# AdaLN block: one DRAM tile for a head's keys, the first two chunks of projections kept on the chip, residuals through TensorE, and a DMA queue in program order

## The chip, the cores and the metric

The kernel runs on one core of a Trainium2 chip. The metric is the device time of one execution in microseconds (us); the time before is the median of six executions. The core has TensorE (PE; its weight loads are listed apart as PEld), VectorE (DVE), ScalarE (ACT) and GpSimd (POOL); SyncE (SP) issues most of the DMA transfers, one after another from its queue.

## The reference

One transformer block with adaptive layer norm over B = 2 sequences of N = 2048 tokens and D = 256 features; H = 16 heads of 16 features each; E = 8 experts.

```python
mod = silu(c) @ wmod                      # six rows of D per sequence
sa, ca, ga, sb, cb, gb = mod              # ga, gb: sign kept, size at least 0.25
h = layernorm(x) * (1 + ca) + sa
q, k, v = h @ Wq, h @ Wk, h @ Wv          # 16 heads of 16
R_hat = (1 + exp(v_h)) / (1 + exp(v_h - w_h * |i - j|))
scores = relu(q k^T) * R_hat              # causal: -inf above the diagonal
x = x + ga * (softmax(scores / 4) v @ Wo + bo)
h = layernorm(x) * (1 + cb) + sb
p = softmax(h @ gate_w^T)                 # 4096 tokens, 8 experts
idx = top 512 tokens of each expert by p
y = layernorm(h[idx]) * ln_w + ln_b
out = (gelu(y @ fc1^T + b1) @ fc2^T + b2) * p[idx]
h[idx] += out                             # scatter-add
x = x + gb * h
```

All of it is float32 except some masks and counts.

## The kernel before

**Start.** A few loads are followed by the first layer norm and the projections of sequence 0, in four chunks of 512 tokens: `prologue(0, c)` lists the steps (load, statistics, normalisation, transposes, projections of k, q and v). Each projected tile is copied out of PSUM by ACT (L513, L530), and stored to DRAM: `k_d[b][i]` and `q_d[b][i]` are 128 x 512 (eight heads of one chunk; i = 4 times the group of eight heads plus the chunk), `v_d` likewise. What a head needs is loaded back from there, spread to partitions 0, 32, 64 and 96 so that four matmuls of 16 rows can run side by side: `keys` (L566) loads four pieces of 16 x 512 for each of four chunks, 16 transfers for a head, `queries` (L606) four of 16 x 512 for each block of 512 queries, `values` (L572) a `vg` tile shared by four heads, and `head_inputs` (L584) the head's distance table `tb` (128 x 2048, from `rhat_d`, which `distances` writes at L363 and L365).

In the program's order: `table = by_distance()`, the first chunk's statistics and normalisation, dummy transposes (`idle`) and the modulation, `narrow()`, `distances(*table)`, chunk 0's projections and loads, chunk 1's normalisation, chunk 1's projections and loads, 20 more dummy transposes, chunk 2's normalisation. The projections of chunks 2 and 3 are fillers, and so is everything else of the start that head 0 does not need. When chunk 3 has arrived, head 1's inputs are asked for, and `late_loads()` loads the output weights, modulation rows and gate weights.

**Attention.** The order of PE, DVE, ACT and POOL is written out by hand by a planner. It keeps a modelled time for each engine, goes over the units (a head and a block of queries) from the first to the last, and puts fillers between their steps: projections of the second sequence, and the epilogues of finished groups of tokens. `there[c]` is the modelled time at which chunk c is usable, `made[...]` the one at which a piece of filler work is finished, `late(i)` says whether the fillers are behind at unit i, and `over()` whether the last scores have been issued. The engine SP is not in the hand-written order: a scheduler places its transfers. Scores are matmuls of L907 into `sc`; DVE multiplies by the table and takes the row maximum (L920, L927), POOL sets the causal part (L932), PE transposes (L971), ACT takes the exponential (L979), PE multiplies by the values (L1012).

**Epilogue of a group of 512 tokens** (`epilogue(b, g)`, pieces for each of four tiles k): `turn` transposes the context (L660, ACT copy at L662), `project` multiplies by Wo (L669) and `add` adds it to the residual `x1`. Once `over()` holds, the addition is made by DVE straight from PSUM (L675). Then come statistics (L690), the normalisation to `h2` (L715, L751), the gate logits (L771 to L783), the row of `z_d` (L788, L792), and the two products of `base`: `h2` times the modulation row and the sum with `x1`, which POOL does (L625), followed by a store to the output (L765).

**Routing and experts.** The top 512 of each expert are found by a bisection over bits of the score's bit pattern: 15 steps, each with three counts on DVE (L1511), one count matmul `pcnt` on PE (L1516) and the comparisons (L1528 and after). Whatever of the epilogues is still undone lies in `left`: its DVE pieces go into the bisection's steps, its POOL pieces are issued by `rest_of_output()` after expert 0's gathers. Then for each expert, POOL gathers 512 rows (L1656, indirect DMA of `zt`), PE transposes (L1671) and does both matmuls (L1682, L1706), and POOL scatter-adds (L1713).

Of the kernel before, what the change touches and what calls it, by code (L numbers as in the profile page):

```python
# [172 lines left out]
def adaln_block_kernel(  # L173
# [30 lines left out]


    q_d = [[dram.tile([P, 512], FP, name=f"q_d_{b}_{i}") for i in range(HG * 4)] for b in range(B)]
    k_d = [[dram.tile([P, 512], FP, name=f"k_d_{b}_{i}") for i in range(HG * 4)] for b in range(B)]
    v_d = [[dram.tile([512, 8 * VW], FP, name=f"v_d_{b}_{i}") for i in range(HG * 4)] for b in range(B)]


# [235 lines left out]
    def prologue(b: int, c: int, hT, first: bool):  # L446
# [56 lines left out]
        def qk(g: int, w_sb, dst, tag: str, parts: list):  # L503
            n = len(parts) * P
            pp = turned([P, n], f"p{tag}_{u}_{g}_{parts[0]}")
            for k in range(DC):
                nc.tensor.matmul(
                    pp, lhsT=w_sb[:, k, ts(g, P)], rhs=s["hT"][:, k, ds(parts[0] * P, n)],
                    start=(k == 0), stop=(k == DC - 1),
                )  # L510
            if parts[0] == 0:
                s[tag, g] = ev_p.tile([P, 512], FP, name=f"{tag}_{u}_{g}", tag="qk")
            nc.scalar.copy(s[tag, g][:, ds(parts[0] * P, n)], pp)  # L513
            if parts[-1] == 3:
                nc.sync.dma_start(out=dst[b][g * 4 + c], in_=s[tag, g])
            return plan.small(427 * len(parts), 120 + 120 * len(parts), 0)

        def val(g: int, parts: list):
            pv = turned([P, len(parts), P], f"pv_{u}_{g}_{parts[0]}")
            for j, i in enumerate(parts):  # L520
                for k in range(DC):
                    nc.tensor.matmul(
                        pv[:, j, :], lhsT=s["hT"][:, k, ts(i, P)], rhs=wv_sb[:, k, ts(g, P)],
                        start=(k == 0), stop=(k == DC - 1),
                    )
            if parts[0] == 0:
                vt = s["v", g] = ev_p.tile([P, 4, 8, VW], FP, name=f"vt_{u}_{g}", tag="vt", bufs=2)
                nc.gpsimd.memset(vt[:, :, :, HD:VW], 1.0)
            vt = s["v", g]
            nc.scalar.copy(  # L530
                vt[:, ds(parts[0], len(parts)), :, 0:HD],
                pv.rearrange("p k (h f) -> p k h f", f=HD),
            )
# [27 lines left out]
        return work  # L561


    def keys(b: int, h: int, c: int):
        for r in range(RG):
            nc.sync.dma_start(  # L566
                out=inputs[b, h][0][ds(32 * r, HD), ts(c, 512)],
                in_=k_d[b][h // 8 * 4 + c][ts(h % 8, HD), :],
            )

    def values(b: int, h: int, c: int):
        nc.sync.dma_start(  # L572
# [3 lines left out]
            ),  # L576
        )

    def head_inputs(b: int, h: int, chunks=range(4)):
        kr = krp.tile([P, N], FP, name=f"kr_{b}_{h}", tag="kr")  # L580

        tb = tabp.tile([P, N], FP, name=f"tb_{b}_{h}", tag="tab")
        row = rhat_d[h, :]
        nc.sync.dma_start(  # L584
            out=tb, in_=bass.AP(tensor=row.tensor, offset=row.offset, ap=[[1, P], [1, N]])
        )

        if h % 4 == 0:
            vg = vgp.tile([P, NQ * 4 * VW + HD], FP, name=f"vg_{b}_{h}", tag="vg")
            nc.gpsimd.memset(vg[:, NQ * 4 * VW :], 0.0)  # L590
        else:
            vg = inputs[b, h - 1][2]
        inputs[b, h] = (kr, tb, vg)
        for c in chunks:
            keys(b, h, c)
            if h % 4 == 0:
                values(b, h, c)

    def queries(at: int):

        if at >= len(asked):
            return
        b, h, c = asked[at]
        qr = qrp.tile([P, 512], FP, name=f"qr_{b}_{h}_{c}", tag="qr")
        for r in range(RG):
            nc.sync.dma_start(  # L606
                out=qr[ds(32 * r, HD), :], in_=q_d[b][h // 8 * 4 + c][ts(h % 8, HD), :]
            )
        qrs[b, h, c] = qr


    def epilogue(b: int, g: int):
# [52 lines left out]

        def project(k: int):
            po = turned([P, D], f"po_{u}_{k}")
            for f in range(HG):
# [12 lines left out]

        def add_to(k: int):
            if ("added", k) in s:
                return 0.0
            x1 = s["x1"][:, k, :]
            return sum_or_product(x1, s["h2"][:, k, :], x1, ALU.add)

# [33 lines left out]
            skip("widen", k)  # L721
            return plan.small(0, 0, 430)

        def skip(name: str, k: int):
            work[:] = [p for p in work if p[3] != (first, name, k)]
            made[first, name, k] = 0.0

        def root():
            s["root"] = root_of(*s["vr", 3], f"3_{u}")
# [18 lines left out]
        def move(k: int):  # L748
            h2 = s["h2"][:, k, :]
            if ("centered", k) in s:  # L750
                nc.vector.scalar_tensor_tensor(  # L751
                    h2, h2, s["rs2"][:, k : k + 1], sb, ALU.mult, ALU.add
                )
                return plan.small(0, 0, 430)
            return sum_or_product(h2, h2, sb, ALU.add)


        def gated(k: int):
# [59 lines left out]
            work[0][4].extend((first - 4, x, k) for x in ("base", "gate") for k in K)  # L818
        for k in K:
            piece("pe", 218, turn, "turn", k, ("project", k - 2) if k > 1 else ("begin", 0))  # L820
            if g == 3 and k < 2:
                work[-1][4].append((first - 2, "gate", k + 2))
            piece("pe", 853, project, "project", k, "turn", "bias")
# [58 lines left out]
    FIRST_OUT = 11  # L882
    SOON = ("load", "bias", "begin", "turn", "project", "add")
    LOW = ("gated", "base", "rows", "stats3", "power3", "root3", "shift3")
    row_free = [0.0, 0.0]
    OPEN = 4
    groups_out = [[epilogue(b, g) for g in range(4)] for b in range(B)]
# [170 lines left out]
    def divide():  # L1058
# [25 lines left out]
        )  # L1084
        plan.small(0, 0, 200 + 150 * gn)
        if h == H - 1:
            add(groups_out[b][gs[0]][1], False)
            i = turns[-1]["i"] if turns else 0
            more(max(i, H * len(PACKS)), FIRST_OUT * len(PACKS) if b < B - 1 else 12)
# [204 lines left out]

    ENG = mybir.EngineType
    behind = {}
    with tc.manual_schedule(engines={ENG.PE, ENG.DVE, ENG.Activation, ENG.Pool}):
        hT0 = cxp.tile([P, 4, DC, 512], FP, name="hT0", tag="ctx")
        ahead = [prologue(0, c, hT0[:, c, :, :], True) for c in range(4)]

# [52 lines left out]
        table = by_distance()  # L1353
        for _, _, w, *_ in ahead[0][1:6]:
            w()
        for _, _, w, *_ in ahead[0][6:11]:
            w()
        idle(40)
        modulation()
        idle(24)  # L1360
        narrow()
        distances(*table)
        head_inputs(0, 0, [])
        plan.start()
        for c in range(4):
# [28 lines left out]
    def weights(e: int):  # L1394
# [28 lines left out]
    def rest_of_output():  # L1423
        for p in left["pool"]:
            assert all(x in done for x in p[4])
            p[2]()
            done.add(p[3])

    with tc.manual_schedule(engines={ENG.PE, ENG.DVE, ENG.Activation, ENG.Pool}):
        b1_sb = rt.tile([P, E * FC], FP, name="b1_sb")  # L1430
# [12 lines left out]
        nc.gpsimd.iota(steps, pattern=[[0, TOP // 2 + 1], [1, 3]], base=1, channel_multiplier=0)  # L1443
        nc.gpsimd.iota(twice, pattern=[[2, TOP // 2 + 1], [0, 3]], base=0, channel_multiplier=0)
        nc.vector.tensor_tensor(steps, steps, twice, ALU.logical_shift_left)
        thr = rt.tile([P, 1], I32, name="thr0", tag="thr", bufs=2)
        nc.vector.memset(thr, 0)

# [58 lines left out]
        for bit in range(TOP, -1, -2):  # L1507
# [9 lines left out]
            if bit:  # L1517
# [22 lines left out]

        while left["dve"]:
            left["dve"].pop(0)()
            ready_rows()

        hit = rt.tile([P, 2, 2, P], FP, name="hit")
        for k, op in ((0, ALU.is_gt), (1, ALU.is_equal)):
# [258 lines left out]
```

## Time and profile before

| what | value |
|---|---|
| six executions | 1734.68, 1736.26, 1731.92, 1741.42, 1749.59, 1736.20 us; median 1736.23 us |
| the profiled execution's own time | 1724.44 us, 0.68% under the median |
| its span on the chip | 1722.7 us |
| mean granted TensorE clock | 0.949 |
| HBM traffic | 105.82 MB read, 25.70 MB written |

The page's sixth part lists the DMA transfers by kind (form, count, size of one, median us from issue to landing):

```profile
kr<-k_d SPq DMA_DIRECT2D x512, 32.0 KB, 1.9
qr<-q_d SPq DMA_DIRECT2D x512, 32.0 KB, 1.9
vg<-v_d SPq DMA_DIRECT2D x32, 136.0 KB, 3.1
```

The 512 transfers of `kr` are 2 sequences x 16 heads x 4 chunks x 4 groups. The timeline of SP's queue in the start shows chunk 0's keys and queries on their way back from DRAM (start, duration, queue, line, form, count):

```profile
19.85 0.45 SPq L515 DMA_DIRECT2D k_d<-k  x1
20.39 0.47 SPq L515 DMA_DIRECT2D q_d<-q  x1
21.30 0.37 SPq L535 DMA_DIRECT2D v_d<-vt  x1
22.90 0.38 SPq L454 DMA_DIRECT2D xt<-in_x_dram  x1
27.25 1.71 SPq L566 DMA_DIRECT2D kr<-k_d  x4
29.01 2.28 SPq L606 DMA_DIRECT2D qr<-q_d  x4
31.33 0.42 SPq L572 DMA_DIRECT2D vg<-v_d  x1
```

### The profile page before, as it was taken

To read this page: it belongs to the slowest core of one execution; us is meant where nothing else is said; L and a number is where in the kernel's file an instruction comes from. 1 tells how busy PE (TensorE), PEld (TensorE's weight loads), DVE (VectorE), ACT (ScalarE), POOL (GpSimd) and SP (SyncE) were. 2 spreads that over 40 slices of the span, in tenths; PEclk is the share of its full clock that TensorE was granted. 3 is DMA by queue.
4 is the path that set the end of the run, shared out by engine and by line. 5 is a ranking of instruction groups with operands and counts; after the bars stand their busy time and mean duration, and the time that the engine had idled before them with its cause. 6 is when DMAs were issued, how large, how long until landed. Compare 5 with 4: busy or idle time off the path is not lost. (4 is left out here: it accounts for less than half of the span.)

```text
span 1722.7 us, 58026 instructions
## 1 busy us (share of the span) xinstructions
PE 1590.1 (92%) x24205; PEld 1114.5 (65%) x24205; DVE 1320.0 (77%) x2533; ACT 839.9 (49%) x2348; POOL 412.1 (24%) x814
## 2 busy tenths in 40 slices
PE   8999999999999999999999999899999943899997
PEld 6677766676766667666666666566666642567674
DVE  5487798888888787788988998789887777654542
ACT  2455665565655556556665565556555521121211
POOL 1111121211111113122231331313311211834342
PEclk9899999999999999899999999999999955999999
DMA  7432232223222222121221322213220031344431
GB/s 229 98 106 83 70 88 70 71 79 103 72 75 76 75 75 82 53 68 54 73 80 51 91 75 73 85 51 96 58 58 5 18 117 34 98 108 119 112 92 22
DMA packets 111285, 135.31 MB, mean 79 GB/s; under 512 B 43312, under 2 KB 81840, under 8 KB 106928
## 3 DMA queue, kind: packets, MB, share of 16 engines
q1 hardware_dynamic: 104880, 123.08, 24.0%
q0 software_dynamic: 6144, 8.52, 2.9%
q8 instruction: 191, 3.13, 0.8%
q14 instruction: 70, 0.57, 0.1%
HBM read 105.82 MB, written 25.70 MB: 76 GB/s over the span
## 5 line engine op out<-in xcount | busy, mean ns | idle before, releaser
L979 ACT ACTIVATE pt<-tr 128x512 f32<-128x512 f32 (+7 forms) x1628 | 632.7, 457 | 489.5 <-PE tr L971 486.3
L920 DVE CUSTOM_DVE_ANT_0 s<-sc,tb 128x128 f32<-128x128 f32 (+15 forms) x512 | 647.4, 1288 | 207.3 <-PE sc L907 186.3
L971 PEld LDWEIGHTS tr<-ident,s 64*128 64x128 f32 x8704 | 343.4, 141 | 234.0 <-issue 94.2
L971 PE MATMUL tr<-ident,s 64*128 64x64 f32 x8704 | 439.0, 234 | 11.5 <-ACT pt L979 6.3
L932 POOL TENSOR_SCALAR_AFFINE_SELECT s<-s 128x128 f32<-128x128 f32 x512 | 171.7, 349 | 1041.3 <-DVE s L927 615.8
L927 DVE TENSOR_SCALAR s<-s,m 128x128 f32<-128x128 f32 (+15 forms) x512 | 392.1, 792 | 9.1
L907 PE MATMUL sc<-kr,qr 16*128 16x384 f32 (+15 forms) x4096 | 360.0, 443 | 27.7 <-DVE m L920 15.5
L1012 PE MATMUL avb<-pt,vg 128*32 128x128 f32 x8704 | 358.0, 284 | 3.6 <-ACT pt L979 2.9
L1012 PEld LDWEIGHTS avb<-pt,vg 128*32 128x32 f32 x8704 | 230.1, 111 | 65.4 <-issue 21.1
L907 PEld LDWEIGHTS sc<-kr,qr 16*128 16x128 f32 x4096 | 161.1, 188 | 85.5 <-DVE m L920 48.5
L1686 ACT ACTIVATE hT<-ph,b_sb 128x512 f32<-128x512 f32 x64 | 43.9, 687 | 182.7 <-PE ph L1682 182.7
L1682 PE MATMUL ph<-yT,w 128*128 128x512 f32 x256 | 116.7, 600 | 0.9 <-DVE yT L1672 0.5
L1706 PE MATMUL pof<-w,hT 128*128 128x256 f32 x512 | 114.3, 382 | 0.0
L1706 PEld LDWEIGHTS pof<-w,hT 128*128 128x128 f32 x512 | 96.8, 191 | 13.1 <-issue 0.5
L1711 DVE TENSOR_TENSOR o<-pof,b2b 128x256 f32<-128x256 f32 x32 | 13.6, 425 | 89.1 <-PE pof L1706 89.1
L1682 PEld LDWEIGHTS ph<-yT,w 128*128 128x128 f32 x256 | 46.8, 190 | 49.2 <-issue 46.2
L1713 POOL DMA_INDIRECT out_dram<-o,idx x32 | 52.2, 1633 | 94.2 <-DVE o L1712 26.2
L625 POOL TENSOR_TENSOR h<-h,modr 128x256 f32<-128x256 f32 x68 | 51.4, 769 | 0.0
L1656 POOL DMA_INDIRECT zt<-z_d,idx x32 | 33.5, 1047 | 66.4 <-issue 48.7
L261 POOL TENSOR_TENSOR rr<-rv,mhalf 128x4 f32<-128x4 f32 x24 | 24.7, 1029 | 90.6 <-DVE rv L260 90.5
L1028 ACT COPY avs<-avb 128x128 f32<-128x128 f32 x128 | 36.1, 282 | 17.2 <-PE avb L1012 16.1
L1046 PE MATMUL trs<-ident,avs 128*128 128x128 f32 x128 | 42.0, 328 | 1.9 <-ACT avs L1028 0.7
(185 smaller groups left out, 1142.6 us busy)
## 6 DMA issues: line engine op xcount, KB each, us to landing
tb<-rhat_d SPq DMA_DIRECT2D x32, 1024.0 KB, 6.3
kr<-k_d SPq DMA_DIRECT2D x512, 32.0 KB, 1.9
qr<-q_d SPq DMA_DIRECT2D x512, 32.0 KB, 1.9
w<-in_fc1T_dram SPq DMA_DIRECT2D x8, 1024.0 KB, 4.8
w<-in_fc2T_dram SPq DMA_DIRECT2D x8, 1024.0 KB, 5.5
v_d<-vt SPq DMA_DIRECT2D x16, 272.0 KB, 2.4
vg<-v_d SPq DMA_DIRECT2D x32, 136.0 KB, 3.1
xt<-in_x_dram SPq DMA_DIRECT2D x8, 512.0 KB, 4.0
```

The costliest lines, as they stand in the source:

```text
L625: nc.gpsimd.tensor_tensor(out, a, c, op)
L907: nc.tensor.matmul(sc[:, r, ds(at, w)], lhsT=qr[ds(32 * r, HD), ts(q % 4, P)], rhs=kr[ds(32 * r, HD), ts(r, w)], start=True, stop=True,)
L920: nc.vector.tensor_tensor_reduce(out=s[:, ds(RG * at, n)].rearrange("p (r w) -> p r w", w=w), in0=sc[:, :, ds(at, w)], in1=rev, scale=1.0, ...
L927: nc.vector.tensor_scalar(s[:, ds(RG * at, n)], s[:, ds(RG * at, n)], 0.0, m[:, j : j + 1], ALU.max, ALU.subtract,)
L932: nc.gpsimd.affine_select(out=diag, in_=diag, pattern=[[-1, P]], compare_op=ALU.is_ge, fill=MASKED, base=0, channel_multiplier=1,)
L971: nc.tensor.transpose(trs[a][:, at + k, :], u["s"][ts(a, TR), ts(k0 + k, P)], ident[ts(a, TR), ts(a, TR)],)
L979: nc.scalar.activation(u["pt"][:, ds(k0, n), ts(a, TR)], trs[a][:, ds(at, n), :], AF.Exp)
L1012: nc.tensor.matmul(avb[ds(32 * j, 32), grp["slot"], :], lhsT=inputs[b, h][2][:, ds((4 * kt + h % 4) * VW, 32)], rhs=u["pt"][:, k, :], star ...
L1682: nc.tensor.matmul(ph, lhsT=s["w"][0][:, k, ts(f, P)], rhs=s["yT"][:, k, :], start=(k == 0), stop=(k == DC - 1),)
L1686: nc.scalar.activation(s["hT"][:, f, :], ph, AF.Gelu_apprx_tanh, bias=b1_sb[:, e * FC + f : e * FC + f + 1])
L1706: nc.tensor.matmul(po, lhsT=s["hT"][:, f, ts(i, P)], rhs=s["w"][1][:, f, :], start=(f == 0), stop=(f == FC - 1),)
L1713: nc.gpsimd.indirect_dma_start(out=outr, out_offset=bass.IndirectOffsetOnAxis(ap=s["idx"][:, i : i + 1], axis=0), in_=o, in_offset=None, b ...
```

## The change

- `k_d` is one DRAM tile of 128 x 2048 for each group of eight heads, and a head's keys come from it in four transfers of 16 x 2048 instead of sixteen of 16 x 512. In head 0 of sequence 0, whose chunks arrive one by one, chunks 2 and 3 still come as 16 x 512.
- For chunks 0 and 1 of sequence 0, group 0, the projected k, q and v go from PSUM straight into head 0's `kr`, `qr` and `vg` (four copies of 16 x 512 for k and for q, alternately by DVE and ACT; one ACT copy for v) beside the store to DRAM, which the other heads use.
- Chunk 1's projections become a filler; the 20 dummy transposes behind them are gone. `distances` moves ahead of the first normalisation.
- SP joins the engines whose order is that of the program.
- In an epilogue after the last scores, the residual is added by one more matmul with the identity, and ACT copies the sum out; DVE's addition is gone.
- The planner knows when a group's context is finished (`made["context", b, g]`), sets an engine's time to that of the latest thing a filler needs, and treats the fillers as late from unit `PAIR_AT` on.
- Seven of the blocks whose `base` is left at the end go from POOL to PE: a diagonal matrix is made of the modulation row, and in the bisection's steps, `base_turned` transposes a block of `h2` and `base_made` multiplies it by the diagonal and adds `x1` by an identity matmul; ACT copies the result out, SP stores it.

```diff
-    k_d = [[dram.tile([P, 512], FP, name=f"k_d_{b}_{i}") for i in range(HG * 4)] for b in range(B)]
+    k_d = [[dram.tile([P, N], FP, name=f"k_d_{b}_{i}") for i in range(HG)] for b in range(B)]
...
+            if first and g == 0 and c < 2:
+
+                if dst is k_d:
+                    to = inputs[0, 0][0][:, ts(c, 512)]
+                else:
+                    to = qrs[0, 0, c] = qrp.tile([P, 512], FP, name=f"qr_0_0_{c}", tag="qr")
+                for r in range(RG):
+                    (nc.scalar.copy if r % 2 else nc.vector.tensor_copy)(
+                        to[ds(32 * r, HD), :], pp[0:HD, :]
+                    )
...
+    def to_groups(dst: bass.AP, src: bass.AP, h: int):
+
         for r in range(RG):
-            nc.sync.dma_start(
-                out=inputs[b, h][0][ds(32 * r, HD), ts(c, 512)],
-                in_=k_d[b][h // 8 * 4 + c][ts(h % 8, HD), :],
-            )
+            nc.sync.dma_start(out=dst[ds(32 * r, HD), :], in_=src[ts(h % 8, HD), :])
+
+    def keys(b: int, h: int, cs: list):
+        n = 512 * len(cs)
+        to_groups(
+            inputs[b, h][0][:, ds(512 * cs[0], n)], k_d[b][h // 8][:, ds(512 * cs[0], n)], h
+        )
...
+            adds = over()
             for f in range(HG):
                 nc.tensor.matmul(
                     po, lhsT=s["cT", k][:, f, :], rhs=wo_sb[:, b, f, :],
-                    start=(f == 0), stop=(f == HG - 1),
+                    start=(f == 0), stop=(f == HG - 1 and not adds),
                 )
-            if over():
-                x1 = s["x1"][:, k, :]
-                nc.vector.tensor_tensor(x1, po, x1, ALU.add)
-                s["added", k] = True
-                return plan.small(853, 0, 350)
+            if adds:
+                nc.tensor.matmul(po, lhsT=ident, rhs=x1, start=False, stop=True)
+            if adds:
+                nc.scalar.copy(x1, po)
+                there = plan.small(853 + 427, 400, 0)
+                skip("add", k, there)
+                return there
...
+        if not w["in_order"]:
+
+            kind = "dve" if over() and p[0] == "pool" and p[3][1] not in LOW else p[0]
+            if kind in ("dve", "act", "pool"):
+                setattr(plan, kind, max([engine(kind)] + [made[x] for x in p[4]]))
...
-        return ahead_by(i) < (1.5 if plan.now == "f" else -1.5)
+        return i >= PAIR_AT or ahead_by(i) < (1.5 if plan.now == "f" else -1.5)
...
-    with tc.manual_schedule(engines={ENG.PE, ENG.DVE, ENG.Activation, ENG.Pool}):
+    with tc.manual_schedule(engines={ENG.PE, ENG.DVE, ENG.Activation, ENG.Pool, ENG.SP}):
...
         def arrived(c: int):
-            keys(0, 0, c)
-            queries(c)
-            values(0, 0, c)
-            there[c] = plan.act + 5000
+            there[c] = max(plan.act, plan.dve) + 200
+            if c > 1:
+                keys(0, 0, [c])
+                queries(c)
+                values(0, 0, c)
+                there[c] = plan.act + 5000
...
         chunk(0)
         normed(1)
-        chunk(1)
-        idle(20)
-        normed(2)
         add(
-            ahead[2][11:13] + [("dma", 0, lambda: normed(3))] + ahead[2][13:25]
+            ahead[1][11:16]
+            + [("dma", 0, lambda: (ahead[3][0][2](), arrived(1), normed(2)) and None)]
+            + ahead[2][11:13] + [("dma", 0, lambda: normed(3))] + ahead[2][13:25]
...
-        "pool": [p for p in pending if p[0] == "pool"],
     }
+    bases = [
+        p[3] for p in pending if p[3][1] == "base" and (p[3][0], "gated", p[3][2]) not in made
+    ][:7]
+    left["pool"] = [
+        p for p in pending if p[0] == "pool" and (p[3][0], "base", p[3][2]) not in bases
+    ]
...
+    def gates_apart():
+        for f in range(DC):
+            nc.vector.tensor_tensor(diag[:, f, :], ident, modr[:, 1, 3, ts(f, P)], ALU.mult)
+
+    def base_turned():
+        if not bases:
+            return
+        first, _, k = bases.pop(0)
+        tr = ps_t.tile([P, DC, P], FP, name=f"trb_{first}_{k}", tag="t")
+        for f in range(DC):
+            nc.tensor.transpose(tr[:, f, :], tiles[first]["h2"][:, k, ts(f, P)], ident)
+        bT = rt.tile([P, DC, P], FP, name=f"bT_{first}_{k}", tag="bT", bufs=2)
+        nc.scalar.copy(bT, tr)
+        half_made.append((first, k, bT))
+
+    def base_made():
...
+        for f in range(DC):
+            nc.tensor.matmul(pb[:, ts(f, P)], lhsT=bT[:, f, :], rhs=diag[:, f, :], start=True, stop=False)
+            nc.tensor.matmul(pb[:, ts(f, P)], lhsT=ident, rhs=x1[:, ts(f, P)], start=False, stop=True)
+        nc.scalar.copy(x1, pb)
+        nc.sync.dma_start(
+            out=outr[ds((first // 4) * N + (4 * (first % 4) + k) * P, P), :], in_=x1
+        )
...
+            if bit % 4:
+                base_made()
+            else:
+                base_turned()
```

More of the change, by code (lines that the diff above doesn't have):

```diff
@@ L512, in qk @@
                 s[tag, g] = ev_p.tile([P, 512], FP, name=f"{tag}_{u}_{g}", tag="qk")
+            if first and g == 0 and c < 2:
[7 more added lines that the diff above has]
+                    )
+                plan.small(0, 0, 1200)
+                plan.small(0, 1100, 0)
             nc.scalar.copy(s[tag, g][:, ds(parts[0] * P, n)], pp)
             if parts[-1] == 3:
-                nc.sync.dma_start(out=dst[b][g * 4 + c], in_=s[tag, g])
+                to = k_d[b][g][:, ts(c, 512)] if dst is k_d else q_d[b][g * 4 + c]
+                nc.sync.dma_start(out=to, in_=s[tag, g])
             return plan.small(427 * len(parts), 120 + 120 * len(parts), 0)
@@ L529, in val @@
             vt = s["v", g]
+            if first and g == 0 and c < 2:
+                vg = inputs[0, 0][2][:, ts(c, 16 * VW)]
+                nc.gpsimd.memset(vg, 1.0)
+                nc.scalar.copy(
+                    vg.rearrange("p (k h f) -> p k h f", h=4, f=VW)[:, :, :, 0:HD],
+                    pv[:, :, 0 : 4 * HD].rearrange("p k (h f) -> p k h f", f=HD),
+                )
+                plan.small(0, 400, 0)
             nc.scalar.copy(
@@ L561, in prologue @@
         return work
-    def keys(b: int, h: int, c: int):
+    def to_groups(dst: bass.AP, src: bass.AP, h: int):
         for r in range(RG):
-            nc.sync.dma_start(
-                out=inputs[b, h][0][ds(32 * r, HD), ts(c, 512)],
-                in_=k_d[b][h // 8 * 4 + c][ts(h % 8, HD), :],
-            )
+            nc.sync.dma_start(out=dst[ds(32 * r, HD), :], in_=src[ts(h % 8, HD), :])
[4 more added lines that the diff above has]
+        )
     def values(b: int, h: int, c: int):
@@ L577, in values, with head_inputs @@
         )
-    def head_inputs(b: int, h: int, chunks=range(4)):
+    def head_inputs(b: int, h: int, chunks=(0, 1, 2, 3)):
         kr = krp.tile([P, N], FP, name=f"kr_{b}_{h}", tag="kr")
@@ L593, in head_inputs @@
         inputs[b, h] = (kr, tb, vg)
[L594 to L597, printed above, removed]
+        if chunks:
+            keys(b, h, chunks)
+        for c in chunks if h % 4 == 0 else []:
+            values(b, h, c)
     def queries(at: int):
@@ L604, in queries @@
         qr = qrp.tile([P, 512], FP, name=f"qr_{b}_{h}_{c}", tag="qr")
[L605 to L608, printed above, removed]
+        to_groups(qr, q_d[b][h // 8 * 4 + c], h)
         qrs[b, h, c] = qr
@@ L667, in project @@
             po = turned([P, D], f"po_{u}_{k}")
+            x1 = s["x1"][:, k, :]
+            adds = over()
             for f in range(HG):
@@ L682, in add_to @@
         def add_to(k: int):
-            if ("added", k) in s:
-                return 0.0
             x1 = s["x1"][:, k, :]
@@ L722, in center, with skip @@
             return plan.small(0, 0, 430)
-        def skip(name: str, k: int):
+        def skip(name: str, k: int, there: float = 0.0):
             work[:] = [p for p in work if p[3] != (first, name, k)]
-            made[first, name, k] = 0.0
+            made[first, name, k] = there
         def root():
@@ L755, in move @@
             return sum_or_product(h2, h2, sb, ALU.add)
+        tiles[first] = s
         def gated(k: int):
@@ L820, in epilogue @@
             piece("pe", 218, turn, "turn", k, ("project", k - 2) if k > 1 else ("begin", 0))
+            work[-1][4].append(("context", b, g))
             if g == 3 and k < 2:
@@ L884, in adaln_block_kernel @@
     LOW = ("gated", "base", "rows", "stats3", "power3", "root3", "shift3")
+    tiles = {}
     row_free = [0.0, 0.0]
@@ L1086, in divide @@
         if h == H - 1:
+            made["context", b, gs[0]] = plan.dve + 150
+            for g in gs[1:]:
+                made["context", b, g] = plan.dve + 150
             add(groups_out[b][gs[0]][1], False)
@@ L1355, in adaln_block_kernel @@
             w()
+        distances(*table)
         for _, _, w, *_ in ahead[0][6:11]:
@@ L1361, in adaln_block_kernel @@
         narrow()
-        distances(*table)
         head_inputs(0, 0, [])
@@ L1427, in rest_of_output @@
             done.add(p[3])
+    diag = rt.tile([P, DC, P], FP, name="diag")
+    half_made = []
+    def gates_apart():
[12 more added lines that the diff above has]
+    def base_made():
+        if not half_made:
+            return
+        first, k, bT = half_made.pop(0)
+        x1 = tiles[first]["x1"][:, k, :]
+        pb = ps_o.tile([P, D], FP, name=f"pb_{first}_{k}", tag="o")
+        for f in range(DC):
[4 more added lines that the diff above has]
+            out=outr[ds((first // 4) * N + (4 * (first % 4) + k) * P, P), :], in_=x1
+        )
     with tc.manual_schedule(engines={ENG.PE, ENG.DVE, ENG.Activation, ENG.Pool}):
@@ L1445, in adaln_block_kernel @@
         nc.vector.tensor_tensor(steps, steps, twice, ALU.logical_shift_left)
+        gates_apart()
         thr = rt.tile([P, 1], I32, name="thr0", tag="thr", bufs=2)
@@ L1538, in adaln_block_kernel @@
             thr = nthr
-        while left["dve"]:
-            left["dve"].pop(0)()
+        while left["dve"] or bases or half_made:
+            if left["dve"]:
+                left["dve"].pop(0)()
             ready_rows()
+            base_turned()
+            base_made()
         hit = rt.tile([P, 2, 2, P], FP, name="hit")
```

## Prediction

> **What bounds the kernel now.** I began with the page's totals and slices.
>
> ```profile
> span 1722.7 us, 58026 instructions
> PE 1590.1 (92%) x24205; PEld 1114.5 (65%) x24205; DVE 1320.0 (77%) x2533; ACT 839.9 (49%) x2348; POOL 412.1 (24%) x814
> PE   8999999999999999999999999899999943899997
> PEclk9899999999999999899999999999999955999999
> ```
>
> PE is busy nearly everywhere, save for two slices near the end (one slice is 43 us) where its clock is halved too. The page's chain of waits holds only the final store, so the bound has to be read stage by stage, from the busy times by stretch (columns: stretch, length, busy time and count of each engine, granted clock, DMA share, GB/s).
>
> ```profile
> 0.00:32.00 32.00, 28.05 (x164) 22.37 (x165) 17.91 (x68) 8.91 (x15) 6.16 (x17) 1.00 0.74 238
> 32.00:98.00 66.00, 59.10 (x707) 45.02 (x709) 36.50 (x65) 27.37 (x81) 8.76 (x22) 0.84 0.47 126
> 98.00:1350.00 1252.00, 1204.42 (x21816) 839.46 (x21812) 1062.05 (x1766) 731.57 (x2110) 271.06 (x655) 0.98 0.24 71
> 1350.00:1399.00 49.00, 41.30 (x363) 32.53 (x363) 31.04 (x101) 18.80 (x62) 7.54 (x12) 0.80 0.29 99
> 1399.00:1442.00 43.00, 9.48 (x32) 7.81 (x32) 36.98 (x219) 5.91 (x12) 5.55 (x12) 0.50 0.13 34
> 1442.00:1493.00 51.00, 35.74 (x193) 24.82 (x194) 35.94 (x70) 8.86 (x13) 31.72 (x37) 0.81 0.18 60
> 1493.00:1500.00 7.00, 1.72 (x7) 0.78 (x6) 0.85 (x2) 0.00 (x0) 5.67 (x5) 0.69 0.73 246
> 1500.00:1722.00 222.00, 210.30 (x933) 141.69 (x933) 98.77 (x244) 38.48 (x56) 75.61 (x55) 0.98 0.38 90
> ```
>
> So: a start of 98 us that the chunks' chain sets, 1252 us of attention at 96% PE, a thin epilogue of 49 us, a bisection of 43 us that DVE sets (86% busy), then routing and experts. Last came the waits: of PE at the start and at the experts, of SP's queue up to 1350 us, and the timeline around the one long PE stall after the bisection.
>
> ```profile
> PE sc L907 <- DMA qr<-q_d: 6.8, 4, 4.0
> PE trf L1671 <- DMA zt<-z_d,idx: 5.3, 2, 5.0
> SPq L606 <- PE sc L907: 374.9, 74, 18.3
> 1485.88 0.49 DVE L1648 SCALAR_TENSOR_TENSOR idx<-pair 128x4 int32<-128x4 f32 x1
> 1492.02 0.72 POOL L625 TENSOR_TENSOR x<-h,x 128x256 f32<-128x256 f32 x1
> 1492.89 1.05 POOL L1656 DMA_INDIRECT zt<-z_d,idx  x1
> 1498.48 1.09 PE L1671 MATMUL trf<-ident,zt 128*128 128x128 f32 x3 [4.99 <-DMA zt<-z_d,idx]
> ```
>
> (First three: total, times, longest.) Expert 1's indices exist at 1486.4 (1485.88 + 0.49), but its gathers start at 1492.89: POOL is emptying a list of 32 operations first. PE pays 5.3 us.
>
> **Part by part.**
>
> Keys in four transfers a head. From 100 to 1345 us the list of PE's waits holds no DMA, so 31 heads' keys arriving with fewer issues are worth 0. Cover: the previous head's scores. Without it, sixteen loads (9.6 us of issue for one head at 100.1 us) would stand against four of 2.4 us, 7 us a head.
>
> [...]
>
> Start. Chunks 0 and 1 no longer go to DRAM and back. Before: k's copy at 17.15, read-back issued 27.25 to 31.3, first scores on PE at 32.0, DVE on them at 33.88. After: distances move ahead of the normalisation (2.5 us of DVE rows, partly in gaps: about +1.0). Each projected tile gets two DVE and two ACT copies of 16x512, issued alternately and, as the semaphores stand, one behind the other. No row has this form; by 512 columns the nearest are 0.69 (DVE, L920) and 0.59 (ACT, L513): 2 x 0.69 + 2 x 0.59 = 2.6, with the hand-overs 2.8 us a tile. Bounds: 1.3 us if the two engines overlap, 4 us with 0.35 us per hand-over. So k at 18.1 + 2.8 = 20.9, q at 23.7, scores then; DVE takes them at about 28.8, behind chunk 1's and 2's statistics (2.1 + 2.0 + 1.4 us each by the rows). That is 5 us earlier, and unit 1 and 2 gain 2 and 6 us. What is late next: chunk 1's projections (7.6 us, 21.2 to 28.8 before) are now filler among the units, and chunk 2, which still makes the round trip, ends about 55 instead of 52.0, its queries are used at 60.8 instead of 58.2, chunk 3's at 80 instead of 78.6. On the other hand the queue no longer sends chunk 3's q behind head 1's seven key loads (q stored at 72.7 after projections done at 71.6; 1 us), and DVE's 9.93 us hole before 81.24 may shrink by what it has less to catch up. Late loads (wo, wm, gate weights; 23 issues, about 0.4 us each, 9 us) now stand before head 1's second query block: chunk 3 at 80, keys 2, late loads 9, four query loads 2.3 and 2 to land make 95, with waits in the queue up to 100, and it is needed at 99.9. Twenty fewer dummy transposes and sixteen fewer warm-ups sat in idle PE time: 0. Net taken: 0, bounds -6 (the 5 us survive, plus 1) to +6 (chunk 3 late by 1.4, loads by 3, copies by 1.6).
>
> Steady attention. The planner's new dependencies only reorder fillers; PE has 1252 - 1204 = 48 us idle in 1252. Taken 0, bounds -4 to +4: a tenth of that idle time either way. SP's waits for buffers (374.9 us in 74) are in the queue, not on PE; in program order their longest, 18.3 us, holds other loads up, but the next block's query lead is larger.
>
> Tail epilogue. Before, after the last head's division at 1376.8, four projections with DVE adds of 0.42 run to 1384.3, then DVE alone for 3.4 us (4 us stretch with PE 0.78 busy), then groups 2 and 3 of the gates at 1387.2 to 1399 on PE, one after another, 5.8 us each at clock 0.50. In the changed order group 2's gating (5.8 us) is interleaved with the projections, and DVE loses four adds (1.7 us). Added: an identity matmul of 128x256, 0.25 us by L669's 1.99/8, times 10 = 2.5 us on PE, four of them here, and ACT copies at 0.42 to 0.59 in the add's place. 22.3 us should become: projections with group 2, 7.5 + 2; group 3's statistics and normalisation 2.3 + 1.3 + 1.7; its gates 5.8, less 2 overlap: about 18.5. Taken -4, bounds -8 (all of the 3.4 + 5.8 less the additions) to +2.
>
> Bisection. Two diagonals on DVE ahead of it: 2 x 0.2 (128x128, half of a 0.42 row) = +0.4. In each step that makes a base, PE gets four 128x128 matmuls. By L771's 1.09 us for four in slow clock plus wider fp32 moving data I take 1 to 2 us, in a gap of about 2 us between a step's two counts (2.56 us a step). Taken +0.4; bounds 0 to +7 (each of seven steps 1 us late). Cover is DVE's own 2 us. A busier PE might raise the clock (0.50), each count matmul then loses 0.25 us of its 0.56: 15 x 0.25 = -3.8, the lower end.
>
> [...] The rows disagree: at 1388 to 1396 PE was 3.93 and 3.96 of 4 us busy, at clock 0.50 throughout. [...]
>
> Gather. Seven of sixteen blocks leave POOL's list: 14 of 32 operations. The list ran 1464.25 to 1492.75, 28.5 / 32 = 0.89 us each: 12.5 us less, so it ends about 1480.3, before the indices at 1486.4. The gathers start 6.4 us earlier and the 4.99 + 0.29 us of waiting goes: -5.3. If the cover is less (the weights' SP queue, scatter stores): 0 to -7 with the clock dip of the 7 us stretch.
>
> Sum: 0 + 0 + 0 - 4 + 0.8 - 5.3 = -8.5. The profiled execution is 1724.44 (span 1722.7), which gives 1715.9; it lies 0.7% under the median 1736.23 of six, on which basis the forecast is 1727.7, written 1728.
>
> **Rivals.**
>
> A, the start's gain survives. For it: DVE's 9.93 us hole and the 4.0 us PE wait. Against: chunks 2 and 3 still go the long way and end later. -6 and the rest: 1728 - 6 - 3 (placement) = 1719.
>
> B, slower: the ordered queue. One mechanism, at the start and at each head: SP's instruction waits at its place for a buffer that PE still reads (18.3 us longest, 374.9 in 74 waits) and everything behind it, stores of a chunk and keys of the next head included, waits too. It decides once a load behind it arrives later than its unit's scores, so where the queue's wait exceeds the lead; at the start that is chunk 3's and head 1's queries. For it: 95 to 100 against 99.9. Against: scheduler's order before also waited in place. Price: one such stall of 10 us in the start and eight of 1.5 in 31 heads, 22 us: 1728 + 22 = 1750.
>
> C, the tail gives it back: the identity matmuls and copies lengthen the serial chain, and base work delays the counts in the bisection (+7), with the gather's gain kept: 0 + 7 - 5.3 + 0.4, about 1738.
>
> D, keys in four is not what is exposed and the other edits each end off the path: 1736.
>
> **How the numbers follow.** The forecast 0.40, A 0.17, B 0.18, C and D 0.25 together. What a measurement can tell from no change is 0.5%, 8.7 us: below 1727.5 is faster, above 1744.9 slower. The forecast sits on the bound: half of its 0.40, somewhat more by A, give faster 0.20 + 0.16 + 0.08 (C and D with a better start) = 0.44; B 0.18 and 0.04 of C give slower 0.22; same 0.34. The range runs from 1710 (A with the tail's lower bound, half-way: 1719 - 4, and the bisection's clock, -4.2 with the diagonals' 0.4 gone) to 1748, just short of B's full price; it leaves about one in ten out on each side.
>
> **What would show it.** Right: the keys' row at 128 KB x124; DVE on the first scores before 30 us; gathers of expert 1 within 1 us of its indices and no PE wait on them; less than 19 us from the last division to the last logits; steps of the bisection still 2.56 us. Wrong: PE waits on DMA in the heads' stretch (B), a start that ends off 97 +- 3 us, or steps over 2.7 us (C).

## The result, and the profile after

The changed kernel is slower: median 1801.79 us of 20 runs against 1738.91 of 46 runs of the kernel before, ratio 1.031 with a 95% interval of 1.0281 to 1.034. The forecast was 1728 (1710 to 1748). The ratio, here and below, compares only the fast executions, those within 1.5% of the fastest of their kernel (median after 1792.96 us), and the profiled execution of 1820.46 us is not one of them. It lies 1% over the median, and that of the kernel before 0.7% under its own, so the two profiles differ by 96 us where the medians differ by 63: what they show of the loss is its place and its kind, not its exact size. A second profile of the same kernel is among the experiments, and the profiles of three variants below, which took 1783 to 1798 us, show the same stops.

The page after (totals, slices and DMA queues):

```profile
span 1818.8 us, 57798 instructions
PE 1682.5 (93%) x24259; PEld 1172.0 (64%) x24259; DVE 1319.4 (73%) x2536; ACT 856.6 (47%) x2383; POOL 399.8 (22%) x800
...
PEclk8889999899999999898895986988799995799999
...
q1 hardware_dynamic: 91408, 122.25, 27.0%
q8 instruction: 192, 3.15, 0.7%
```

PE does 54 more matmuls of 24,205 and is busy 92 us longer. DVE is busy as long as before. So the same matmuls run slower, and the clock row shows 5 to 8 tenths in slices of the attention where it showed 8 to 9. The busy times by stretch (same columns as before):

```profile
0.00:32.00 32.00, 25.40 (x153) 19.63 (x154) 18.05 (x66) 9.73 (x17) 5.58 (x18) 0.86 0.54 178
32.00:102.00 70.00, 65.24 (x671) 46.09 (x669) 40.00 (x76) 32.14 (x93) 9.68 (x24) 0.82 0.37 97
102.00:1457.00 1355.00, 1280.08 (x21832) 885.60 (x21828) 1062.86 (x1766) 734.36 (x2111) 269.41 (x653) 0.92 0.29 67
1457.00:1506.00 49.00, 40.45 (x386) 33.49 (x382) 31.63 (x106) 23.20 (x73) 10.56 (x18) 0.88 0.30 101
1506.00:1545.00 39.00, 25.65 (x100) 20.93 (x100) 33.74 (x206) 9.86 (x23) 3.13 (x7) 0.50 0.21 55
1545.00:1597.00 52.00, 35.90 (x193) 24.99 (x194) 33.76 (x74) 8.86 (x13) 27.21 (x28) 0.80 0.25 80
1597.00:1818.00 221.00, 209.82 (x939) 141.30 (x937) 99.40 (x246) 38.50 (x56) 74.27 (x55) 0.99 0.37 90
```

The attention took 1355 us instead of 1252, with the granted clock 0.92 instead of 0.98; everything behind it is a little shorter than before, as forecast. The whole loss, and more, lies in the start (4 us by these stretches) and above all in the attention, the parts that the prediction put at 0. What PE waited for there (total, times, longest):

```profile
PE tr L999 <- issue: 16.2, 10, 4.0
PE sc L935 <- DVE m L948: 14.0, 44, 0.7
PE avb L1040 <- issue: 8.3, 6, 2.1
PE sc L935 <- DMA qr<-q_d: 6.4, 1, 6.4
PE sc L935 <- issue: 5.3, 2, 3.0
```

Before, "issue" stood there with two lines:

```profile
PE tr L971 <- issue: 3.4, 2, 2.1
PE sc L907 <- issue: 1.2, 1, 1.2
```

"issue" is a wait for nothing that the profile's semaphores show: no tile was late, yet PE stopped. One such stop, with the four microseconds ahead of it, from the timeline of PE (start, duration, line, form, count):

```profile
477.78 0.82 PE L935 MATMUL sc<-kr,qr 16*128 16x320 f32 x8
478.53 0.71 PE L999 MATMUL tr<-ident,s 64*128 64x64 f32 x16
479.17 0.52 PE L1040 MATMUL avb<-pt,vg 128*32 128x128 f32 x9
481.58 0.42 PE L1040 MATMUL avb<-pt,vg 128*32 128x128 f32 x5 [1.89 <-issue]
```

The stop falls inside a run of 14 equal matmuls. The timeline of SP's queue just before it:

```profile
470.10 0.37 SPq L609 DMA_DIRECT2D tb<-rhat_d  x1
470.51 1.94 SPq L588 DMA_DIRECT2D kr<-k_d  x4
472.55 4.94 SPq L588 DMA_DIRECT2D qr<-q_d  x4
```

And the DMA queues in the stretch from 472 to 478 us (packets, MB, share of 16 engines):

```profile
q1 hardware_dynamic: 217, 1.24, 98.9%
```

and from 478 to 481 us:

```profile
q1 hardware_dynamic: 146, 0.16, 45.7%
q8 instruction: 1, 0.02, 3.7%
```

The table (1 MB) and the four key transfers (0.5 MB) of the next head are issued within 2.3 us and keep all 16 engines full until about 479 us. Queue q8 moves 16 KB at a time, 192 times in the run; 48,518 PE instructions (24,259 matmuls and as many weight loads) over 192 are 253 each, and 256.1 with the 659 other instructions of PE in the trace. So these packets are PE's own program, fetched a block at a time. The one here starts at 478.3 and ends 1.5 us before PE goes on at 481.58; the one before it had started at 466.5, 11.8 us earlier. In the attention they start 7.2 us apart (median, before). Counted over the traces, in the attention alone (half-clock time is the time at a granted clock of 0.50):

```
                         before   after   second profile of after
fetches over 11 us apart      7      22      19
PE stops of 1 us or more
  that end 1.1 to 1.9 us
  after a fetch has landed    3      15      14
  and their sum, us         4.6    30.5    25.5
half-clock time, us          58     229     225
last scores end, us      1350.0  1457.2  1446.3
```

15 of the 18 stops of that length end so. The clock makes the larger part of the loss. In the attention of the trace after, PE did 2,397 matmuls in 222.4 busy us at clock 0.50 and 19,427 in 1057.7 busy us in the rest: 10.8 and 18.4 a microsecond, a rate of 0.59. At that rate (229 - 58) x 0.41 = 70 us, an estimate. PE's idle time in the attention grew from 47.6 to 74.9 us, 27 more. 70 + 27 = 97, against the measured 107 (1457.2 - 1350.0); some 10 us are open.

### The profile page after: what moved, and what is told of

Its sections match the earlier page's. It is cut to its first block, busy times and chain, and to the rows that moved or that the text cites. A ratio compares the mean times of both kernels' runs of the same rounds, so it can differ in the third digit from the quotient of the medians.

```text
span 1818.8 us, 57798 instructions
## 1 busy us (share of the span) xinstructions
PE 1682.5 (93%) x24259; PEld 1172.0 (64%) x24259; DVE 1319.4 (73%) x2536; ACT 856.6 (47%) x2383; POOL 399.8 (22%) x800
## 5 line engine op out<-in xcount | busy, mean ns | idle before, releaser
L999 PEld LDWEIGHTS tr<-ident,s 64*128 64x128 f32 x8704 | 359.7, 148 | 262.9 <-issue 118.9
L999 PE MATMUL tr<-ident,s 64*128 64x64 f32 x8704 | 459.4, 241 | 29.6 <-issue 16.2
L935 PE MATMUL sc<-kr,qr 16*128 16x32 f32 (+15 forms) x4096 | 385.5, 465 | 29.4 <-DVE m L948 14.0
L1040 PE MATMUL avb<-pt,vg 128*32 128x128 f32 x8704 | 377.9, 293 | 12.5 <-issue 8.3
L1040 PEld LDWEIGHTS avb<-pt,vg 128*32 128x32 f32 x8704 | 241.0, 115 | 83.4 <-issue 38.0
L935 PEld LDWEIGHTS sc<-kr,qr 16*128 16x128 f32 x4096 | 171.9, 197 | 92.1 <-DVE m L948 41.6
L1056 ACT COPY avs<-avb 128x128 f32<-128x128 f32 x128 | 35.9, 281 | 23.9 <-PE avb L1040 23.2
L507 PE MATMUL pq<-hT,wq_sb 128*128 128x128 f32 (+1 forms) x232 | 44.9, 332 | 1.3 <-ACT pt L1007 0.5
L647 POOL TENSOR_TENSOR h<-h,modr 128x256 f32<-128x256 f32 x60 | 45.4, 770 | 0.1
```

What stands on the lines that cost most here:

```text
L507: nc.tensor.matmul(pp, lhsT=w_sb[:, k, ts(g, P)], rhs=s["hT"][:, k, ds(parts[0] * P, n)], start=(k == 0), stop=(k == DC - 1),)
L647: nc.gpsimd.tensor_tensor(out, a, c, op)
L935: nc.tensor.matmul(sc[:, r, ds(at, w)], lhsT=qr[ds(32 * r, HD), ts(q % 4, P)], rhs=kr[ds(32 * r, HD), ts(r, w)], start=True, stop=True,)
L999: nc.tensor.transpose(trs[a][:, at + k, :], u["s"][ts(a, TR), ts(k0 + k, P)], ident[ts(a, TR), ts(a, TR)],)
L1040: nc.tensor.matmul(avb[ds(32 * j, 32), grp["slot"], :], lhsT=inputs[b, h][2][:, ds((4 * kt + h % 4) * VW, 32)], rhs=u["pt"][:, k, :], star ...
```

## The experiments

Theory F at first: the key transfers alone, by their rows of 8 KB, make the fetches late. Rival Q: the ordered queue makes data late.

**The changed kernel without the ordered queue.**

```diff
-    with tc.manual_schedule(engines={ENG.PE, ENG.DVE, ENG.Activation, ENG.Pool, ENG.SP}):
+    with tc.manual_schedule(engines={ENG.PE, ENG.DVE, ENG.Activation, ENG.Pool}):
```

> The changed kernel, but the DMA queue is left to the scheduler again (SyncE is not in the hand-made order). Theory F (the keys' rows of 8 KB right behind the table's 1 MB fill the DMA engines for some 10 us, TensorE's next 16 KB of instructions come late, it stops for 1 to 4 us, and the clock halves after it): the burst stays, so about 1790 us, 10 or more TensorE stops that end 1.2 to 1.5 us after a fetch of instructions lands, and most of the attention's half-clock time of 230 us is kept. Rival Q (the queue in program order makes the loads wait and the cores of the stall are late data): about 1735 us and few stops.

Measured: median 1735.21 us, ratio to the kernel before 0.9963 (0.9919 to 1.0007). Seven stops at a fetch, 10.0 us; half clock for 99 us. Against F.

**The changed kernel with sixteen key transfers a head.**

```diff
-        n = 512 * len(cs)
-        to_groups(
-            inputs[b, h][0][:, ds(512 * cs[0], n)], k_d[b][h // 8][:, ds(512 * cs[0], n)], h
-        )
+        for c in cs:
+            to_groups(inputs[b, h][0][:, ts(c, 512)], k_d[b][h // 8][:, ts(c, 512)], h)
```

> The changed kernel, but a head's keys come again in sixteen transfers of 16x512, rows of 2 KB, in the same queue order. Theory F: the stops go but for one or two, half-clock time in the attention falls from 230 us to about 70, and the time to 1720 to 1740 us. Rival Q: sixteen issues in a fixed order make the queue's waits longer, so 1795 us or more.

Measured: 1737.99 us, 0.9996 (0.997 to 1.0022), no stop at a fetch. The time is as F said, and against Q; but half clock stays at 126 us, where F said about 70, and PE waits once, for 9.2 us, for queries that come late.

**The kernel before with four key transfers a head, nothing else.**

```diff
...
-        for c in chunks:
-            keys(b, h, c)
+        if chunks:
+            keys(b, h, 0, 4)
+        for c in chunks:
```

> The kernel before, with a head's keys in four transfers of 16x2048 and nothing else. Theory F: about 1790 us (1.03), with 10 or more stops that end at a fetch. Rival Q: 1730 to 1740 us, no more than three such stops.

Measured: 1751.80 us, 1.0057 (1.0023 to 1.0092), five stops, 11.9 us. Far under what F asked, and above Q's range.

**The kernel before with the queue in program order, nothing else.**

```diff
-    with tc.manual_schedule(engines={ENG.PE, ENG.DVE, ENG.Activation, ENG.Pool}):
+    with tc.manual_schedule(engines={ENG.PE, ENG.DVE, ENG.Activation, ENG.Pool, ENG.SP}):
```

> The kernel before, with the DMA queue in program order and nothing else. Theory F: 1730 to 1750 us (the late loads ahead of head 1's queries may cost one stop of some us). Rival Q: about 1790 us.

Measured: 1754.76 us, 1.0078 (1.0041 to 1.0116), two stops, 2.6 us. Neither edit alone makes the loss, and undoing either one removes it: both theories fall. In the trace of SP's queue, the sixteen transfers take 10 us to issue, and left to the scheduler the four big ones stand 3.3, 3.8, 4.2 and 7.2 us behind the table (medians). Only the two edits together put 1.5 MB into the engines within some 2 us. That is theory B, the burst.

**The kernel before with both.** The two edits above together.

> The kernel before with both: keys in four transfers and the DMA queue in program order; nothing else. Theory B (the two together make it: in program order a head's table, 1 MB, and its four key transfers, 0.5 MB, are issued within 2 us, and TensorE's next 16 KB of instructions wait behind this burst): more than the sum of the two alone, 1795 to 1815 us, 8 or more stops that end at a fetch, half-clock time in the attention over 180 us. Rival P (some other part of the change, the planner's bookkeeping say, makes the rest): the sum of the two alone, 1741 + 11 + 14 = about 1766 us.

Measured: 1849.70 us, ratio 1.0626 (1.0519 to 1.0733); 18 stops, 45.6 us, half clock for 263 us. The two make the loss without the rest of the change, and a larger one than B's 1795 to 1815 us.

**The changed kernel with the late loads spread.**

```diff
...
-            late_loads()
+            loads = late_loads()
+            for j in range(0, len(loads), 3):
+                behind.setdefault(len(PACKS) + 1 + j // 3, []).extend(loads[j : j + 3])
```

> The changed kernel, with the 23 late loads (output weights, modulation and gate weights) issued three at a time in the units of head 1 instead of all at once ahead of its second query block. Theory B: the stop of 6 to 9 us near 100 us and the half clock behind it go, head 2 starts 10 to 18 us earlier, the burst at each head stays: 1780 to 1792 us. Rival P: the start is the whole loss and it falls to about 1740 us.

Measured: 1789.24 us, 1.0304 (1.0211 to 1.0398). Twelve stops, 23.2 us, remain. Head 2's first scores come at 142.9 us instead of 152.9 (second profile of the changed kernel: 148.9). In the queue of the changed kernel the late loads are what stands between head 1's keys and its second query block:

```profile
84.03 1.94 SPq L588 DMA_DIRECT2D kr<-k_d  x4
86.02 0.97 SPq L386 DMA_DIRECT2D wm<-in_wmod_dram  x2
87.03 15.30 SPq L390 DMA_DIRECT2D wo_sb<-in_wo_dram  x16
```

The sixteen loads of `wo_sb` take 15.3 us, and the queries that PE waits 6.4 us for are issued at 106.8. This is a second, smaller loss: the ratio hardly moves here (1.0304 after 1.031), and it stands out of the noise only in the last experiment. The bursts stay, and with them the larger loss.

**The changed kernel with the keys apart from the table.** The table stays at the head's second unit; the keys, and the values of every fourth head, move to the unit of query tile 10.

```diff
-                        head_inputs(*divmod(nh, H))
+                        head_inputs(*divmod(nh, H), (0, 1, 2, 3) if qs != [4, 5] else ())
+                if qs == [10] and 1 < b * H + h + 1 < B * H:
+                    nb, nh = divmod(b * H + h + 1, H)
+                    if (b, h) != PAIR[0]:
+                        keys(nb, nh, (0, 1, 2, 3))
+                        for c in range(4) if nh % 4 == 0 else []:
+                            values(nb, nh, c)
```

> The changed kernel, with a head's four key transfers issued some three units (about 8 to 12 us) after its table instead of right behind it; same transfers, same rows, same order otherwise. Theory B: the burst is cut in two, late fetches fall from 26 to under 12 with at most two stops, 1735 to 1752 us. Rival R (rows of 8 KB written to 16 partitions hold the DMA engines, wherever they stand): 1775 us or more.

Measured: 1722.01 us, 0.9968 (0.9925 to 1.0012) and no stop at a fetch, faster even than B's range; it was 1.031 with the same transfers in the same form. Fetches over 11 us apart fall from 22 to four; the 26 of the expectation is another count, not that of the table above. The first key transfer is issued 8.75 us behind the table (median) instead of 0.41. PE's waits in the attention no longer name "issue":

```profile
PE sc L935 <- DVE m L948: 16.3, 50, 0.7
PE tr L999 <- ACT pt L1007: 4.6, 10, 0.7
PE avb L1040 <- ACT pt L1007: 3.6, 9, 1.0
PE sc L935 <- DMA qr<-q_d: 2.6, 1, 2.6
```

**The changed kernel with rows of 2 KB in the same four transfers.**

```diff
-    k_d = [[dram.tile([P, N], FP, name=f"k_d_{b}_{i}") for i in range(HG)] for b in range(B)]
+    k_d = [[dram.tile([P, 4, 528], FP, name=f"k_d_{b}_{i}") for i in range(HG)] for b in range(B)]
...
+            inputs[b, h][0][:, ds(512 * cs[0], n)].rearrange("p (c n) -> p c n", n=512),
+            k_d[b][h // 8][:, ds(cs[0], len(cs)), 0:512], h,
...
```

> The changed kernel, with a gap of 16 columns behind each 512 in the DRAM tile of the keys, so that each of the four transfers moves 64 rows of 2 KB instead of 16 rows of 8 KB; same bytes, same four issues within 2 us. Theory B (bytes that stand before the fetch): as the changed kernel, 1785 to 1810 us. Rival R (the size of a row): 1730 to 1750 us.

Measured: 1786.75 us, 1.0275 (1.0183 to 1.0368), eleven stops, 20.4 us. The size of the keys' rows is not the cause; the table's rows were 8 KB in every run.

**Bytes that nobody reads.** The kernel with the keys apart, and behind each table four transfers of 16x2048 into partitions 16 to 31 of each group of the key tile, which no instruction reads.

```diff
+                        if qs == [4, 5]:
+                            nb, n1 = divmod(nh, H)
+                            for r in range(RG):
+                                nc.sync.dma_start(
+                                    out=inputs[nb, n1][0][ds(32 * r + HD, HD), :],
+                                    in_=k_d[nb][n1 // 8][ts(n1 % 8, HD), :],
+                                )
```

> The kernel with the keys three units apart, and right behind each table four more transfers of 16x2048 into partitions of the key tile that nothing reads: 0.5 MB a head that nobody waits for. Theory B: the late fetches come back (over 18) with stops that end at a fetch, 1775 to 1800 us, although no data are later. Rival T (the loss is from keys or queries that arrive late): as without them, 1720 to 1735 us.

Measured: 1801.27 us (four runs, 1776.03 to 1809.54) beside 1742.90 of the kernel before on the same chip (eleven, 1728.38 to 1749.43); the medians stand at 1.033, and the lowest of the four lies above the highest of the eleven. Eleven stops, 22.2 us, 16 fetches over 11 us apart, and half clock for 208 us, where the kernel with the keys apart has no stop, four such fetches and 55 us. The waits in the attention are those of the changed kernel again:

```profile
PE tr L999 <- issue: 11.7, 7, 2.3
PE sc L935 <- issue: 6.9, 3, 4.3
PE avb L1040 <- issue: 6.5, 4, 2.2
```

No needed load was moved, and half a megabyte a head that nobody waits for costs about what the change cost. This rules out late keys as the cause.

**Keys one unit behind the table.** The edit, against the kernel with the keys apart:

```diff
-                if qs == [10] and 1 < b * H + h + 1 < B * H:
+                if qs == [6, 7] and 1 < b * H + h + 1 < B * H:
```

> The changed kernel with a head's keys one unit (2 to 3 us) after its table instead of three. The table needs about 6 us to land, so under theory B most of the burst is still one: 1745 to 1785 us, between the changed kernel and the keys three units apart, late fetches between 9 and 26. Rival S (it is the issues standing back to back in the queue, not the bytes in flight): 1720 to 1730 us.

Measured: 1788.24 us, 1.025 (1.0182 to 1.0317), thirteen stops. It tells nothing of a smaller distance: the table itself waits in SP's queue for the buffer that DVE still reads, so that the keys were issued 0.41 us behind it, as in the changed kernel. On rival S another run speaks: with sixteen transfers in program order, seven of them (0.22 MB) stand back to back behind the table within 3.2 us (medians), and PE has no stop at a fetch. So issues back to back do not make the loss without the bytes.

**The changed kernel again.**

> The changed kernel once more, for a second profile beside these three. Theory B and its rivals alike: 1775 to 1820 us; under theory B 8 or more stops that end 1.2 to 1.5 us after a fetch lands, and over 170 us of half clock in the attention.

Measured: 1809.59 us; its counts stand in the table above.

**Both repairs: keys apart and late loads spread.**

> The changed kernel with both repairs: a head's keys three units after its table, and the late loads three at a time in head 1. Theory B: the gain of the late loads measured before (12 us) comes on top of the 1722 us of the keys apart: 1705 to 1716 us, faster than both kernels by more than 1%. Rival P (the two repairs mend the same thing): 1720 us or more.

Measured: 1713.50 us beside 1742.90, ratio 0.9834 (0.9794 to 0.9875): faster than both kernels. No stop at a fetch, two fetches over 11 us apart, and head 2 at 137.0 us instead of 149.4 with the keys apart alone. Its page:

```profile
span 1710.2 us, 57807 instructions
PE 1610.0 (94%) x24259; PEld 1130.6 (66%) x24259; DVE 1318.4 (77%) x2536; ACT 854.3 (50%) x2383; POOL 400.6 (23%) x800
```

## Why the prediction was wrong

**The step that failed** is "Keys in four transfers a head ... worth 0", with "Steady attention ... Taken 0, bounds -4 to +4". Both asked who waits for the moved transfers and found nobody, which was right and stayed right. They did not ask what else the 16 DMA engines carry. PE's program comes over them too (q8: 192 packets of 16 KB, 0.7% of the engines' time), and a fetch has a due time like any tile. The trace shows that time. Take the number of instructions that PE has begun when a fetch starts, less 256 for each fetch before it: it is mostly 160 to 250 (median 207 before, 213 after). At each of the 15 stops, and at the three before, PE stood at 449 or 450 by this count, whatever instruction came next: by my reading it had run dry. The fetches behind these 15 stops had started at 353 to 449, and every fetch that started later than 406 brought a stop. From 213 that is 140 to 193 instructions, so at 7.2 us for 256 a fetch may start some 4 to 5.5 us late, an estimate, before PE stops.

The table took 6.3 us to land before; table and keys together took 10.9 us from the first issue to the last landing (median after; 15.5 before, but spread over 10 us of issues, with room between them). This span alone does not decide: sixteen transfers in program order took 12.0 us and made no stop at a fetch, four in the scheduler's order 10.4 us and made seven. By these runs the bytes must also stand close together.

The measured price of the step, taken together with the ordered queue, is +94 us in the profile (head 2's first scores to the last: 1210.3 to 1304.3 us), and +87 in the second one. The sum had a second term wrong, the start, "Net taken: 0, bounds -6 ... to +6": head 2 began 13.2 us later (9.2 in the second profile).

The signs were in the profile before: the page's line "q8 instruction: 191, 3.13, 0.8%", and among PE's waits three stops on "issue" of 1.2 to 2.1 us, each just after a fetch.

By these counts a block is 16 KB and 256.1 instructions, and the next one is fetched while PE still has instructions: some 236 of them, 449 less 213, at a fetch's usual start. In the kernel before, this left 4.6 us of stops at a fetch; here it left 30.5 us, beside 229 us at half clock.

**The keys' merging** was worth 0 by the row, which missed its cost. Joined transfers alone gained nothing here and cost 0.6% (1.0057); the harm came where they stood right behind another large one (1.0626 with both edits).

**Rival B, the ordered queue,** had the place right at the start and the mechanism wrong elsewhere. Its "needed at 99.9, landing 95 to 100" came as queries issued at 106.8, a stop of 6.4 us and half clock from 108.5 to 122.1: head 2 starts at 152.9 instead of 139.7. With the queue free (first experiment) it starts at 132.1. What was mis-sized are the late loads, "about 0.4 us each, 9 us": the 23 of them held the queue for 20 us (86.02 to 106.21), 8.6 us of it in waits of the `wo_sb` loads for earlier transfers to land. A row before had shown five `wo_sb` loads taking 4.88 us. "One such stall in the start and eight of 1.5 in 31 heads" by late data did not occur; after the start no head waits for its data.

**Start.** Scores on PE at 23.1 us (forecast 23.7), DVE on them at 29.6 (28.8); the copies are 0.68 us on DVE, alternating with ACT, as taken. The 5 us survived, and more, where nothing else took them: -7.6 us at head 2 with a free queue. The net of 0 was two effects of opposite sign, about 8 us won and 21 lost to the ordered queue (152.9 against 132.1 in the changed kernel; in the kernel before 151.5 against 139.7, 12 us), each taken too small.

**Tail epilogue.** Last scores to last logits 45.0 us after 49.0 before: -4.0, forecast -4. The number came by luck. The forecast saw the gain behind the last head's division, and there it is nil: 21.6 us to the last logits after 21.7 (DVE's write of `ctx` ends at 1480.54 and 1377.25), not under 19, and PE still waits 4.0 us for DVE ahead of the last gates (3.4 before). The 4 us were won ahead of the division, 23.4 us from the last scores after 27.3; no run here takes apart why.

**Bisection.** From its first count matmul to its last 36.6 us after 36.0: +0.6, forecast +0.8 with the diagonals ahead of it. The clock stayed at 0.50, as the row had it, with PE busy 25.65 of 39 us, in pieces, after 9.48 of 43 before.

**Gather.** POOL's list ends before the indices of expert 1 are there and the gathers follow at once:

```profile
1584.98 0.73 POOL L647 TENSOR_TENSOR x<-h,x 128x256 f32<-128x256 f32 x1
1588.09 1.06 POOL L1741 DMA_INDIRECT zt<-z_d,idx  x1 [2.38 <-DVE second L1737]
```

PE has no wait on them. From the last count matmul to the end: 274.0 us after 281.8, -7.8, forecast -5.3 with -7 as the end of its range. Of the rest, some 2 us are the half clock from 1495.6 to 1502.4 around the old stop, which I had named and not counted: PE's first eight transposes of the expert and the 16 matmuls behind them took 2.42 and 4.35 us there, and 1.04 and 3.62 us now, at clock 1.00. The last 0.5 us is open.

So the terms behind the attention came to -11.2 us, forecast -8.5, the tail's by luck, and were swamped by the attention's term, which the sum had at 0.

## What to carry to other kernels

Before bunching DMA transfers, add up what will be in flight at once, and ask how long it keeps the engines full beside what the busiest engine's instruction fetches can bear, here, by the estimate above, a delay of some 4 to 5.5 us in a cadence of 7.2: here loads that nobody waits for stopped an engine that had all its data (eleven stops, 22.2 us, with the unread bytes). No run here measured a threshold: 1 MB with the keys 8.75 us behind it made no stop, 1.5 MB issued within 2 to 3 us made 11 to 18. A wait on "issue" in the middle of a run of equal instructions, one to two microseconds after a packet of the instruction queue, was the sign here. Two edits that cost little each (0.6% and 0.8%) made 6% together, so undo them one by one and together.

## What the runs showed of the hardware

In the changed kernel ten of the 15 stops at a fetch (1.2 to 4.0 us each) were followed, within 2 us or so of their end, by 3.4 to 44 us at half clock, 133 us in all. The other five were not, among them one of 2.1 us at 298.4, one of 1.65 at 435.6 and one of 1.89 at 479.7. Of the 229 us at half clock, 72 have no stop of 1 us just ahead of them, so what else sets the clock is open.

Why a fetch of one 16 KB packet starts late behind a burst of another queue is open. The trace shows that it does (at 478.3, 11.8 us after the one before, with queue q1 on 98.9% of the engines' time from 472 to 478), and the runs show that the loss stays with rows of 2 KB in the keys (1.0275) and goes with the same bytes 8.75 us later (0.9968). What sets the order of the two queues is not in the trace. Open too is why both edits in the kernel before cost more (1.063, 45.6 us of stops) than in the changed kernel (1.031, 30.5 us): some 11 us are the gains at the tail and the gather, the rest was not tried.
